# Four layers on one core: the small experts' gate and up weights as the stationary operand, and memsets on POOL between the transfers of five spreads

## The chip, the cores and the metric

The kernel runs on one core of a Trainium2 chip. The metric is the device time of one execution in microseconds; three executions of the kernel before took 1931.96, 1932.44 and 1936.04 us, so the median is 1932.44 us. The engines are named as in the profile: PE multiplies matrices, PEld is its loading of the stationary operand, DVE and ACT work on vectors, POOL issues the indirect transfers, SP issues the plain ones.

## What is computed

The reference is a network of four layers on x of 4 x 1024 x 128 in f32. Each layer has a token mixer and a feed-forward part, with a layer norm after each. What matters here are the routed parts of the second and fourth layer (L1 and L3), whose experts are small: 128 x 128 for gate, up and down. L2 routes too, with larger experts; it shares the transfers.

```python
# L1: 16 experts, 4 of a token, from the best groups
topk_idx, tw = _route(x, router_w, bias)
combine = (one_hot(topk_idx, 16) * tw[..., None]).sum(1)
h = einsum('td,edf->etf', x, gate_w)
u = einsum('td,edf->etf', x, up_w)
y = einsum('etf,efd->etd', silu(h) * u, down_w)
routed = einsum('etd,te->td', y, combine)
...
# L3: 32 experts, 4 of a token
h = silu(einsum('nd,ehd->neh', flat, gate_w)) * einsum('nd,ehd->neh', flat, up_w)
expert_out = einsum('neh,edh->ned', h, down_w)
sel = take_along_axis(expert_out, topk_idx[:, :, None], axis=1)
out = (sel * topk_scores[:, :, None]).sum(axis=1)
```

Both add a dense shared expert, and L2 routes every token to 2 of 8 experts.

## The kernel before

**Parts.** The 4096 tokens stand in SBUF as 32 tiles of 128. A routed layer takes them in parts: L1 as `a` and `r` (16 tiles each), L2 as `a` (16), `m` and `n` (8 each), L3 as `a` (16), `b` and `c` (8 each). "l1r" below is L1's part r.

**A routed part has four steps.** The router and `positions` give every pair of token and expert a row in a list sorted by expert, where each tile of 128 rows has one expert; the tiles' experts are the integers `ids`. `spread` (L1373) writes each tile of x to its rows in HBM: per tile and choice one indirect transfer from POOL, so 64 for 16 tiles of 4 choices and 32 for 8 tiles of 4 or 16 of 2. `small_experts` (L1781) goes through the list in groups of four tiles. `collect` (L1441) gathers the results back with indirect transfers (`yt`), and DVE adds them into x with the router's weight (L1452).

**A group of the small experts.** `gathered` loads four tiles of rows with SP (`xg`), and waits for all transfers of the spread. PE transposes them (`tp`), ACT copies that out (`xgT`). In `up`, PE reads the four experts' numbers into registers, and multiplies with the tile `xgT` stationary and 256 columns of the weights moving: gate and up of one tile in one product (`gu`, tokens on the partitions). ACT takes silu of the gate half (`sg`), DVE multiplies with the up half (`hg`). `turn` transposes `hg` on PE, DVE copies that out (`hT`, L173). `down` multiplies `hT` with the down weights (`yp`), ACT or DVE copies out (`yg`), and SP writes to the list of results. The weights of all experts of a layer lie in SBUF (`wall`, in the trace `ld`), loaded long before their use. Groups are pipelined: `up(g+1)`, `turn(g)`, `inputs(g+2)`, `down(g-1)` in one turn of the loop. There are 18 groups in l1a, 18 in l1r, 20 in l3a, 12 in l3b and 12 in l3c. A list can be longer than these; `rest_of` puts the further groups behind a branch on its length.

**What sets the order.** Each stage is a generator that yields its estimated time; `mix` (L242) runs a main one and a side one together, and sets the side's instructions in each engine's queue behind the latest of the main's. So the small experts of l1a run beside L0's and L1's work on the other half of the tokens, those of l1r beside L2's routing and the l2a spread, those of l3a beside L3's mixer for b, its routing and its spread, those of l3b and l3c beside the gathers of the part before.[...]

**The spreads that wait.** Under `spaced(..., 1, 2, 1.45)` an indirect transfer waits until the one two before it has landed (`before`, L1345), and the plan reckons 1.45 us for each. This holds for the spreads of l1r, l2a, l2m, l2n and l3a, and for some gathers; the spreads of l1a, l3b and l3c are not spaced. `indirect` (L1325) also keeps each transfer behind the last two of other lists on POOL (`self.moved`).

Of the kernel before, what the change touches and what calls it, by code (L numbers as in the profile page):

```python
# [14 lines left out]
AF = mybir.ActivationFunctionType  # L15
ALU = mybir.AluOpType
# [4 lines left out]
P = 128  # L21
# [3 lines left out]
BLK = 512  # L25
# [49 lines left out]
class Kernel:  # L75
    def __init__(self, ctx, tc, ins, out, cols, consts, rows):
        self.tc, self.nc, self.ins, self.out = tc, tc.nc, ins, out
        self.count = itertools.count()
        nc = self.nc
        self.const = self.pool(ctx, "const")  # L80
        self.small = self.pool(ctx, "small", 3)
        self.routes = self.pool(ctx, "routes")
        self.side = self.pool(ctx, "side", 2, space=PSUM)
        dram = self.pool(ctx, "dram", space=DRAM)

        self.cols_t = self.load(self.const, ins["cols"])
        self.cst_t = self.load(self.const, ins["consts"])
        self.x = self.tile(self.const, [P, NT, D], "x")
        self.xT = self.tile(self.const, [P, NT * P], "xT")
        nrow = ins["rows"].shape[1]  # L90
        self.rows_t = self.tile(self.const, [P, nrow], "rows")
        nc.gpsimd.dma_start(out=self.rows_t, in_=ins["rows"].to_broadcast([P, nrow]))
        self.col = {k: self.cols_t[:, a:b] for k, (a, b) in cols.items()}
        self.cst = {k: self.cst_t[:, a:b] for k, (a, b) in consts.items()}
        self.row = {k: self.rows_t[:, a:b] for k, (a, b) in rows.items()}
        self.ident = self.cst["ident"]
        self.eps = self.tile(self.const, [P, 1], "eps")
        nc.vector.memset(self.eps, LN_EPS)
# [1274 lines left out]
    def spread(self, lay, part, k):  # L1373

        pos, _, _, done, _ = self.route[lay + part.name]
        rows = self.lists[lay, part.name][0]
        for t in range(part.nt):
            for i in range(k):
                ins = self.indirect(
                    apart=done,  # L1380
                    out=rows, out_offset=bass.IndirectOffsetOnAxis(ap=pos[:, t, i : i + 1], axis=0),
                    in_=self.x[:, part.order[t], :], in_offset=None,
                )
                done.append(ins)
            yield (self.step * k,)
        self.listed.add(lay + part.name)

# [11 lines left out]
            )  # L1399
        return xg  # L1400

    def experts_of(self, ids, g, ne):
        _, es = self.nc.values_load_multi_w_load_instructions(
            ids[0:1, g * 4 : g * 4 + 4], engines=[mybir.EngineType.PE], min_val=0, max_val=ne - 1,
            skip_runtime_bounds_check_because="clamped to the last expert",
        )
        return es
# [370 lines left out]
        cp = self.pool(ctx, "l1fw")  # L1778
        return self.load(cp, self.ins["l1_w"])

    def small_experts(self, lay, ne, part, wall, held=None):  # L1781

        nc = self.nc
        pos, wk, ids, done, used = self.route[lay + part.name]
# [2 lines left out]
        with ExitStack() as ctx:  # L1787
            gp = self.pool(ctx, lay + "fg" + part.name, 3)
            ps = self.pool(ctx, lay + "fpe" + part.name, 2, space=PSUM)
            ng = tl // 4  # L1790
            xgTs, ess, hs, hTs = {}, {}, {}, {}

            def inputs(g):
                xg = self.gathered(gp, rows, g, done, part.nt * K3)
                xgTs[g] = self.tile(gp, [P, BLK], "xgT")
                self.transposes(ps, xgTs[g], [xg[:, i, :] for i in range(4)], on_act=True, tag="tp")

            def up(g):
                es = ess[g] = self.experts_of(ids, g, ne)
                xgT = xgTs.pop(g)  # L1800
                h = hs[g] = self.tile(gp, [P, 4, P], "hg")
                for c in range(2):
                    pg = self.tile(ps, [P, 2, 2, P], "gu")
                    for i in range(2):
                        self.mm(
                            pg[:, i].rearrange("p a f -> p (a f)"),
                            xgT[:, (2 * c + i) * P : (2 * c + i + 1) * P],
                            wall[:, bass.ds(es[2 * c + i] * (3 * P), 2 * P)],
                        )
                    sg = self.tile(gp, [P, 2, P], "sg")  # L1810
                    nc.scalar.activation(sg, pg[:, :, 0, :], AF.Silu)  # L1811
                    nc.vector.tensor_tensor(h[:, 2 * c : 2 * c + 2, :], sg, pg[:, :, 1, :], ALU.mult)  # L1812

            def turn(g):
                h = hs.pop(g)
                hT = hTs[g] = self.tile(gp, [P, BLK], "hT")
                self.transposes(ps, hT, [h[:, i, :] for i in range(4)], on_act=False, tag="tp")

            def down(g):
                es, hT = ess.pop(g), hTs.pop(g)  # L1820
# [12 lines left out]
                return marks  # L1833

            def rest(g):
                inputs(g)
                up(g)
                turn(g)
                down(g)


            inputs(0)
            inputs(1)
            up(0)
            for g in range(ng + 1):
                if g + 1 < ng:
                    up(g + 1)
                if g < ng:
                    turn(g)
                if g + 2 < ng:  # L1850
                    inputs(g + 2)
                marks = down(g - 1) if g else ()
                if g == ng:
                    while held and (got := self.queued(held)):
# [368 lines left out]
```

## Time and profile before

| | us |
|---|---|
| median of three executions | 1932.44 |
| the profiled execution | 1937.33 |
| its span, first to last instruction | 1935.5 |
| busy: PE, DVE, ACT, POOL | 1541.5, 1199.2, 900.6, 690.3 |
| l1a experts: first row loaded to last product | about 366 to 457 |
| l1r experts | about 746 to 836 |
| l3a experts | about 1596 to 1712 |
| l3b experts | about 1743 to 1796 |
| l3c experts | about 1816 to 1869 |

The granted PE clock was 0.896 over the whole. A row of a group gives the line, the engine, the operation, what it writes and reads, the count, the busy time and the mean of one; `x8` on a timeline row means eight of the kind one after the other. An f32 product appears as two records on PE. A line can be that of a helper: L161 is every product, L169 every transpose, L1327 every indirect transfer. In brackets stands how long the engine was idle before, and what released it. POOLq, ACTq, PEldq and SPq are the sequencers of these engines: register loads, branches and transfers' issues.

### The profile page before, as it was taken

What the parts mean: (1) busy time and instruction counts of PE and PEld (TensorE: products, weight loads), DVE (VectorE), ACT (ScalarE), POOL (GpSimd) and SP (SyncE); (2) the same over time, 40 slices, a digit from 0 to 9 for tenths busy, and PEclk for the clock granted to TensorE, in tenths of its full rate; (3) what the DMA queues carried; (4) which work ended last, traced back from release to release, by engine and by line L of the source; (5) the groups of instructions that cost most, each with busy time, mean ns of one, the idle gap of its engine ahead of it and who ended that gap; (6) DMA issues with size and microseconds to landing.
All of it is one profiled execution on the core that took longest, in us unless ns stands there. A gap on an engine that the chain in (4) does not pass through costs nothing. (4 is left out here: it accounts for less than half of the span.)

```text
span 1935.5 us, 27095 instructions
## 1 busy us (share of the span) xinstructions
PE 1541.5 (80%) x9025; PEld 920.8 (48%) x9025; DVE 1199.2 (62%) x3491; ACT 900.6 (47%) x1349; POOL 690.3 (36%) x670
## 2 busy tenths in 40 slices
PE   7885677597847887989977878798798998999850
PEld 3332433385423345856632232333355757768650
DVE  8998698465766664635564565546442446866383
ACT  5876265243324554423336756564532236644330
POOL 2000148604630660265443000030536430567775
PEclk9897688798978998999988988898988999989985
DMA  9990002244430113632241000000452213425452
GB/s 297 288 288 10 1 17 86 87 126 133 159 129 18 60 63 129 183 96 73 78 137 32 1 1 1 2 23 1 159 213 83 66 28 93 141 68 167 122 147 61
DMA packets 215530, 187.10 MB, mean 97 GB/s; under 512 B 16528, under 2 KB 194064, under 8 KB 214864
## 3 DMA queue, kind: packets, MB, share of 16 engines
q1 hardware_dynamic: 194672, 142.29, 23.6%
q0 software_dynamic: 20704, 42.86, 7.3%
q8 instruction: 84, 1.38, 0.3%
q14 instruction: 70, 0.57, 0.1%
HBM read 88.49 MB, written 96.60 MB: 96 GB/s over the span
## 5 line engine op out<-in xcount | busy, mean ns | idle before, releaser
L1081 ACT ACTIVATE pr<-sc 128x1024 f32<-128x1024 f32 x288 | 279.4, 1021 | 175.2 <-PE sc L161 174.8
L161 PE MATMUL sc<-qm,kT 32*128 32x512 f32 (+3 forms) x1536 | 197.7, 559 | 16.7 <-ACT pr L1081 16.7
L161 PE MATMUL s<-pr,va 128*32 128x512 f32 (+3 forms) x1536 | 167.5, 532 | 19.0 <-DVE x L1019 10.2
L161 PE MATMUL gu<-ld,xgT 128*128 x640 | 165.1, 400 | 10.2 <-DVE hg L1812 5.9
L1087 DVE TENSOR_TENSOR pr<-pr,ld 128x512 f32<-128x512 f32 (+1 forms) x160 | 91.7, 581 | 105.6 <-ACT pr L1081 105.4
L161 PE MATMUL gu<-wall,xgT 128*128 x304 | 148.2, 612 | 2.0 <-ACT xgT L171 2.0
L161 PEld LDWEIGHTS sc<-qm,kT 32*128 32x128 f32 x1536 | 83.7, 194 | 112.4 <-issue 61.1
L161 PEld LDWEIGHTS gu<-ld,xgT 128*128 128x128 f32 x640 | 119.5, 198 | 34.7 <-DVE hg L1812 6.1
L1812 DVE TENSOR_TENSOR hg<-sg,gu 128x256 f32<-128x256 f32 x160 | 66.0, 417 | 92.0 <-ACT sg L1811 91.6
L173 DVE COPY hT<-tp 128x512 f32<-128x512 f32 x118 | 80.9, 686 | 66.2 <-PE tp L169 66.2
L1567 ACT ACTIVATE sg<-gu 128x512 f32<-128x512 f32 x76 | 45.4, 597 | 144.7 <-PE gu L161 143.6
L1811 ACT ACTIVATE sg<-gu 128x256 f32<-128x256 f32 x160 | 61.3, 385 | 107.7 <-PE gu L161 79.8
L171 ACT COPY xgT<-tp 128x512 f32<-128x512 f32 x99 | 58.0, 586 | 99.9 <-PE tp L169 99.8
L1327 POOL DMA_INDIRECT l1ra<-x,posl1a x64 | 79.8, 1246 | 61.3 <-DVE peq L1321 42.0
L1327 POOL DMA_INDIRECT l1rr<-x,posl1r x64 | 65.4, 1022 | 100.9 <-DVE posl1r L1302 70.8
L169 PEld LDWEIGHTS tp<-ld,hg 128*128 128x128 f32 x624 | 77.4, 141 | 49.0 <-issue 32.5
L1569 DVE TENSOR_TENSOR hg<-sg,gu 128x512 f32<-128x512 f32 x76 | 51.8, 682 | 78.9 <-ACT sg L1567 78.8
L1327 POOL DMA_INDIRECT l2rm<-x,posl2m x16 | 15.7, 983 | 236.8 <-DVE peq L1320 230.1
L169 PE MATMUL tp<-ld,hg 128*128 128x128 f32 x624 | 96.4, 275 | 3.7 <-DVE hg L1812 2.0
L1327 POOL DMA_INDIRECT l3ra<-x,posl3a x64 | 63.7, 996 | 93.3 <-DVE usedl3a L1315 51.0
L161 PEld LDWEIGHTS s<-pr,va 128*32 128x32 f32 x1536 | 37.1, 113 | 122.6 <-issue 78.4
L161 PE MATMUL yp<-ld,hT 128*128 x640 | 86.1, 276 | 2.3 <-DVE mv L197 1.5
(447 smaller groups left out, 3439.1 us busy)
## 6 DMA issues: line engine op xcount, KB each, us to landing
wall<-wall SPq DMA_DIRECT2D x16, 768.0 KB, 7.8
l3ra<-zero SPq DMA_DIRECT2D x1, 6144.0 KB, 25.5
ld<-in_l_w SPq DMA_DIRECT2D x2, 3072.0 KB, 10.6
wall<-we SPq DMA_DIRECT2D x24, 256.0 KB, 2.1
ld<-in_l_w SPq DMA_DIRECT2D x1, 6144.0 KB, 20.6
l1ra<-zero SPq DMA_DIRECT2D x1, 5120.0 KB, 19.6
l1rr<-zero SPq DMA_DIRECT2D x1, 5120.0 KB, 23.1
xg<-l3ra SPq DMA_DIRECT2D x20, 256.0 KB, 2.9
```

Of the source, the lines that this page charges most:

```text
L161: return self.nc.tensor.matmul(out, lhsT, rhs, start=start, stop=stop)
L169: nc.tensor.transpose(pt[:, k * P : (k + 1) * P], s, self.ident)
L171: nc.scalar.copy(dst, pt[:, : n * P])
L173: nc.vector.tensor_copy(dst, pt[:, : n * P])
L1081: nc.scalar.activation(pr, sc[h], AF.Exp)
L1087: nc.vector.tensor_tensor(d, d, cst["tril"].unsqueeze(1).unsqueeze(1).to_broadcast([P, 2, n, P]), ALU.mult)
L1327: ins = self.nc.gpsimd.indirect_dma_start(**kw)
L1567: nc.scalar.activation(sg, gu[:, 0, :], AF.Silu)
L1569: nc.vector.tensor_tensor(h, sg, gu[:, 1, :], ALU.mult)
L1811: nc.scalar.activation(sg, pg[:, :, 0, :], AF.Silu)
L1812: nc.vector.tensor_tensor(h[:, 2 * c : 2 * c + 2, :], sg, pg[:, :, 1, :], ALU.mult)
```

## The change

There are two parts. In the small experts of L1 and L3, gate and up swap operands. A new step `held(g)` copies the gate and up weights of a group's four experts out of `wall` into a tile `wc` of 128 x 4 x 256 (three buffers): the first two with ACT, the other two with DVE, each after reading its two experts' numbers into its own registers. `up` then multiplies with 128 columns of `wc` stationary and the tile `xgT` moving, once for gate and once for up, so that features come out on the partitions, and the result has the layout that `down` needs: `turn`, its transposes and its copy are gone. The loop has one turn less, and `held` runs two groups ahead. PE reads the experts' numbers in `up` as before, and uses them in `down` alone.

In `spread`, when it is spaced, a memset of a 128 x 384 tile of bytes on POOL follows each transfer, and is entered in `self.moved`, so that later transfers queue behind it. Nothing reads the tile.

```diff
+        self.idle = self.tile(self.const, [P, 384], "idle", mybir.dt.uint8)
...
                 done.append(ins)
+                if self.spacing:
+                    stay = self.nc.gpsimd.memset(self.idle, 0)
+                    self.tc.add_manual_dep(
+                        stay.ins, ins.ins.name,
+                        mybir.DependencyInfo(mybir.DependencyClass.NoSync, mybir.DependencyReason.DATA),
+                        reason="queued behind",
+                    )
+                    self.moved.append(stay.ins.name)
             yield (self.step * k,)
...
-    def experts_of(self, ids, g, ne):
+    def experts_of(self, ids, g, ne, engine=mybir.EngineType.PE, first=0, count=4):
         _, es = self.nc.values_load_multi_w_load_instructions(
-            ids[0:1, g * 4 : g * 4 + 4], engines=[mybir.EngineType.PE], min_val=0, max_val=ne - 1,
+            ids[0:1, g * 4 + first : g * 4 + first + count], engines=[engine], min_val=0, max_val=ne - 1,
...
+            def held(g):
+
+                wc = wcs[g] = self.tile(gp, [P, 4, 2 * P], "wc", bufs=3)
+                for n, (eng, copy) in enumerate((
+                    (mybir.EngineType.Activation, nc.scalar.copy), (mybir.EngineType.DVE, nc.vector.tensor_copy),
+                )):
+                    es = self.experts_of(ids, g, ne, eng, 2 * n, 2)
+                    for i in range(2):
+                        copy(wc[:, 2 * n + i, :], wall[:, bass.ds(es[i] * (3 * P), 2 * P)])
+
             def up(g):
                 es = ess[g] = self.experts_of(ids, g, ne)
+                wc = wcs.pop(g)
...
                     for i in range(2):
-                        self.mm(
-                            pg[:, i].rearrange("p a f -> p (a f)"),
-                            xgT[:, (2 * c + i) * P : (2 * c + i + 1) * P],
-                            wall[:, bass.ds(es[2 * c + i] * (3 * P), 2 * P)],
-                        )
+                        for j in range(2):
+                            self.mm(
+                                pg[:, j, i, :], wc[:, 2 * c + i, j * P : (j + 1) * P],
+                                xgT[:, (2 * c + i) * P : (2 * c + i + 1) * P],
+                            )
                     sg = self.tile(gp, [P, 2, P], "sg")
-                    nc.scalar.activation(sg, pg[:, :, 0, :], AF.Silu)
-                    nc.vector.tensor_tensor(h[:, 2 * c : 2 * c + 2, :], sg, pg[:, :, 1, :], ALU.mult)
-
-            def turn(g):
-                h = hs.pop(g)
-                hT = hTs[g] = self.tile(gp, [P, BLK], "hT")
-                self.transposes(ps, hT, [h[:, i, :] for i in range(4)], on_act=False, tag="tp")
+                    nc.scalar.activation(sg, pg[:, 0], AF.Silu)
+                    nc.vector.tensor_tensor(h[:, 2 * c : 2 * c + 2, :], sg, pg[:, 1], ALU.mult)
...
-                    pm = self.mm(py[:, i, :], hT[:, i * P : (i + 1) * P], wall[:, bass.ds(es[i] * (3 * P) + 2 * P, P)])
+                    pm = self.mm(py[:, i, :], h[:, i, :], wall[:, bass.ds(es[i] * (3 * P) + 2 * P, P)])
...
+            held(0)
+            held(1)
             inputs(0)
             inputs(1)
             up(0)
-            for g in range(ng + 1):
+            for g in range(ng):
+                if g + 2 < ng:
+                    held(g + 2)
                 if g + 1 < ng:
                     up(g + 1)
-                if g < ng:
-                    turn(g)
                 if g + 2 < ng:
                     inputs(g + 2)
-                marks = down(g - 1) if g else ()
-                if g == ng:
+                marks = down(g)
+                if g + 1 == ng:
```

More of the change, by code (lines that the diff above doesn't have):

```diff
@@ L1779, in l1_wall, with small_experts @@
         return self.load(cp, self.ins["l1_w"])
-    def small_experts(self, lay, ne, part, wall, held=None):
+    def small_experts(self, lay, ne, part, wall, ahead=None):
         nc = self.nc
@@ L1790, in small_experts @@
             ng = tl // 4
-            xgTs, ess, hs, hTs = {}, {}, {}, {}
+            xgTs, ess, hs, wcs = {}, {}, {}, {}
             def inputs(g):
@@ L1804, in up @@
                     for i in range(2):
-                        self.mm(
-                            pg[:, i].rearrange("p a f -> p (a f)"),
-                            xgT[:, (2 * c + i) * P : (2 * c + i + 1) * P],
-                            wall[:, bass.ds(es[2 * c + i] * (3 * P), 2 * P)],
-                        )
-                    sg = self.tile(gp, [P, 2, P], "sg")
-                    nc.scalar.activation(sg, pg[:, :, 0, :], AF.Silu)
-                    nc.vector.tensor_tensor(h[:, 2 * c : 2 * c + 2, :], sg, pg[:, :, 1, :], ALU.mult)
-            def turn(g):
-                h = hs.pop(g)
-                hT = hTs[g] = self.tile(gp, [P, BLK], "hT")
-                self.transposes(ps, hT, [h[:, i, :] for i in range(4)], on_act=False, tag="tp")
+                        for j in range(2):
[3 more added lines that the diff above has]
+                            )
+                    sg = self.tile(gp, [P, 2, P], "sg")
+                    nc.scalar.activation(sg, pg[:, 0], AF.Silu)
+                    nc.vector.tensor_tensor(h[:, 2 * c : 2 * c + 2, :], sg, pg[:, 1], ALU.mult)
             def down(g):
-                es, hT = ess.pop(g), hTs.pop(g)
+                es, h = ess.pop(g), hs.pop(g)
                 py = self.tile(ps, [P, 4, D], "yp")
                 for i in range(4):
-                    pm = self.mm(py[:, i, :], hT[:, i * P : (i + 1) * P], wall[:, bass.ds(es[i] * (3 * P) + 2 * P, P)])
+                    pm = self.mm(py[:, i, :], h[:, i, :], wall[:, bass.ds(es[i] * (3 * P) + 2 * P, P)])
                 yg = self.tile(gp, [P, 4, D], "yg")
@@ L1835, in rest @@
             def rest(g):
+                held(g)
                 inputs(g)
                 up(g)
-                turn(g)
                 down(g)
+            held(0)
+            held(1)
             inputs(0)
@@ L1844, in small_experts @@
             up(0)
-            for g in range(ng + 1):
+            for g in range(ng):
+                if g + 2 < ng:
+                    held(g + 2)
                 if g + 1 < ng:
                     up(g + 1)
-                if g < ng:
-                    turn(g)
                 if g + 2 < ng:
                     inputs(g + 2)
-                marks = down(g - 1) if g else ()
-                if g == ng:
-                    while held and (got := self.queued(held)):
+                marks = down(g)
+                if g + 1 == ng:
+                    while ahead and (got := self.queued(ahead)):
                         self.now += got[0]
```

## The prediction

> **What bounds the kernel now.** I read the table of busy time by stage first, cut at the first and last row of each list of experts, since the change touches only those stages and the spreads. Its columns are the stretch, its length, busy time of PE, PE's weight loads, DVE, ACT and POOL, then granted clock, DMA share and GB/s.
>
> ```profile
> 366.00:458.00 92.00, 78.38 (x504) 69.58 (x504) 62.15 (x135) 32.84 (x69) 17.68 (x8) 0.93 0.35 104
> 746.00:836.00 90.00, 75.06 (x457) 66.28 (x457) 49.68 (x196) 34.39 (x69) 18.20 (x19) 0.92 0.60 190
> 1596.00:1712.00 116.00, 103.42 (x620) 83.73 (x620) 86.92 (x294) 70.51 (x137) 35.01 (x32) 0.98 0.38 113
> 1743.00:1796.00 53.00, 47.95 (x296) 41.80 (x295) 30.94 (x76) 24.50 (x50) 40.37 (x42) 0.97 0.58 171
> 1816.00:1869.00 53.00, 45.41 (x288) 40.53 (x288) 30.49 (x84) 24.95 (x50) 38.91 (x41) 0.97 0.64 171
> 1869.00:1936.00 67.00, 0.00 (x0) 0.00 (x0) 34.50 (x153) 2.08 (x7) 39.89 (x38) 0.51 0.27 72
> ```
>
> The five stages are l1a, l1r, l3a, l3b and l3c with 18, 18, 20, 12 and 12 groups. PE is the fullest engine in each; in the last 67 us it does nothing. One steady group of l3a on PE (start, length, instruction):
>
> ```profile
> 1648.81 1.97 PE L161 MATMUL gu<-ld,xgT 128*128 x8
> 1650.61 0.60 PE L169 MATMUL tp<-ld,hg 128*128 128x128 f32 x4
> 1651.05 0.60 PE L169 MATMUL tp<-ld,xg 128*128 128x128 f32 x4
> 1651.48 1.06 PE L161 MATMUL yp<-ld,hT 128*128 x8
> 1652.38 0.43 PE L161 MATMUL gu<-ld,xgT 128*128 x1
> ```
>
> From start to start: gate and up 1.80 us, the transposes of h 0.44, those of the input 0.43, down 0.90: 3.57 us a group, no gap. Each f32 product is two records.
>
> Whether a stage's gain reaches the end depends on POOL, which issues every scatter and gather. At the end of l1r:
>
> ```profile
> 854.42 0.96 POOL L1327 DMA_INDIRECT l2ra<-x,posl2a  x1 [0.30 <-DMA l2ra<-x,posl2a]
> 859.60 4.01 SPq L1392 DMA_DIRECT2D xg<-l2ra  x3
> 860.41 1.83 PE L161 MATMUL py<-ld,hs 128*128 128x128 f32 x14 [0.63 <-DVE hs L764]
> 862.58 0.63 PE L169 MATMUL tp<-ld,xg 128*128 128x128 f32 x4 [0.34 <-DMA xg<-l2ra]
> ```
>
> PE ends its last product before l2's first experts at 862.2 and waits 0.34 us for rows whose scatter ended just before: PE and the l2a spread are in balance there. And at the end of the kernel, the gathers of l3:
>
> ```profile
> L1327 POOL DMA_INDIRECT yt<-l3ya,posl3a x64: 943/945/1185, 1712.8 to 1833.7; - x64
> L1327 POOL DMA_INDIRECT yt<-l3yb,posl3b x32: 943/945/1003, 1836.4 to 1875.3; - x32
> L1327 POOL DMA_INDIRECT yt<-l3yc,posl3c x32: 944/945/3440, 1877.6 to 1920.3; - x32
> ```
>
> With the 32 scatters of l3c between them these are 160 transfers in 207.5 us, 1.30 each, where 0.96 of work and 0.30 of issue make 1.26. From 1712.8 on POOL is the bound, and it starts when l3a is made. So a faster l3b or l3c is worth nothing; an earlier end of l3a moves the end one for one.
>
> **The change part by part.**
>
> *PE.* Gate and up become 16 records of 128 columns in place of 8 of 256. Down is 8 such records in 0.90 us, weight loads hidden, so 16 take 1.80: nothing gained or lost. The four transposes of h go: 0.44 us a group, and with them DVE's copy hT (0.69 us, 128x512 from PSUM) and its two hand-overs. A PE-bound group goes from 3.57 to 3.13 us.
>
> *The copies.* ACT gets two 128x256 copies a group: its row on SBUF of that size is `lg`, 0.42 us; so 0.83. DVE gets two; its copies of 128x256 elements (`sv`, `em`) take 0.29, so 0.59, less than the 0.69 that leaves. Each engine also reads two expert numbers into registers, once a group. PE reads four such in these rows:
>
> ```profile
> L1403 PEldq TENSOR_LOAD <-idsl3a x20: 328/332/792, 1600.1 to 1698.2; - x20
> L1418 ACTq TENSOR_LOAD <-usedl1a x1: 467/467/467, 455.2 to 455.2; - x1
> ```
>
> [...] I take the row, and half of that load as hidden, since at 455.2 ACT's load ran under its copy yg. The copies are made one or two groups ahead of their use, so they reach PE only where ACT's or DVE's queue is full.
>
> *l1a.* PE is full in nearly all of it: 18 x 0.44 = 7.9, less two groups that stand at a bump, plus about 0.6 of shorter drain: 7.5 us. The gathers of l1ya start as soon as l1a ends (459.3, after waiting for its writes), so this passes on.
>
> *l1r.* The first seven groups are held by transfers: the second-layer weights load with DMA at 0.60 of the stage. The other eleven save 11 x 0.44 = 4.8. But the l2a spread starts behind about five of them on DVE, so some 2 us earlier; PE then waits for it. Before the memsets the stage is worth 2, not 4.8.
>
> *l3a.* 20 x 0.44 = 8.8 if PE bound it throughout. In these two slices ACT does, and gets 0.83 to 1.2 us a group in about four groups, 4.5 us:
>
> ```profile
> 1634.00:1644.00 10.00, 7.80 (x46) 6.60 (x45) 3.92 (x11) 8.34 (x14) 0.00 (x0) 0.83 0.18 52
> 1664.00:1674.00 10.00, 6.74 (x44) 5.57 (x44) 7.27 (x22) 9.48 (x20) 7.56 (x9) 1.00 0.59 173
> ```
>
> I take +4, between -2 (ACT late everywhere) and +9.
>
> *The memsets.* 192 on POOL, one behind each transfer of the five spreads that wait for landings (l1r 64, l2a 32, l2m and l2n 16 each, l3a 64). No row has 384 one-byte elements; the nearest are POOL's `zero`, 128 elements, 0.23 us, and `keep`, 1024, 0.96: 0.83 ns an element, so 0.42 us by elements, 0.18 if four bytes go at once. What a transfer then costs more lies between 0.06 (the memset fills the 0.30 us of issue) and 0.45 (it stands beside it). For a lower end, POOL's memset `zero` at the start overlapped the DMA behind it by 0.09 us. I take 0.15. Most of it is covered: these transfers already wait for the landing two before. Going through the starts in the rows and lengthening only steps that no landing set, l1r's 64 end 6.5 us later (22 at 0.45), l2a's 32 end 0.9 later (4.9), l3a's and l2n's 80 end 2.9 later (10.8). Cover: l1r's last lands 19 us before its first rows are loaded at 745.5, l3a's some 88 us before 1596. l2a has none: 2 - 0.9 leaves 1. A gain from a memset has no row to speak for it; I put it at nothing.
>
> [...]
>
> **Sum**, on the profiled execution's own time of 1937.3 us (span 1935.5 and 1.8 around it): 7.5 + 1 + 4 - 1.5 = 11, so 1926.3. That execution lay 4.9 us above the median of the runs; the same 11 off 1932.4 gives 1921.4, rounded to 1921.5.
>
> **The rivals.**
>
> *POOL falls behind its plan* (slower). At 0.45 a memset, l1r's spread ends 22 us later against 19 of cover: 3 lost. The l2a spread ends 4.9 - 2 = 3 late, and PE waits for it. The l3a spread ends 10.8 late, and with it the gathers of l2m behind it in POOL's queue (1508.6 to 1531.4); their adds stand on DVE from 1526 to 1536 ahead of the experts' products, which then wait up to 10. With 1.5 at the end that is 17.5 against gains of 11.5: 1938.5. It decides from about 0.40 a memset. For it: nothing in the plan's step of 1.45 us a transfer allows for a memset, and what a memset costs between two transfers has no row. Against: the cover named above.
>
> *ACT takes it back* (no change). If its load and copies are exposed in all 20 groups of l3a (22 us on 70.5 busy, in a queue that PE waits on), l3a gives -2 and l1a's 7.5 is halved by late input copies: 1932.4 - 3.7 + 2 + 1.5 - 1 = 1931. Against: ACT has 33 of 92 us in l1a.
>
> *All of it passes* (faster still): 7.9 + 4.8 + 8.8, nothing lost at the end, the l2a spread earlier with the experts: 1911. For it: the chain from h to down loses a copy and a PE pass, so PE's short gaps close too. Against: the balance at 862.
>
> **How the numbers follow.** Likeliest case 0.55, 1921.5, its own range 1914 to 1928. POOL behind 0.20; ACT 0.13; all of it 0.12. What can be told from no change is 0.2%, 3.9 us, so the ACT case counts as the same. Faster: 0.53 of the likeliest, 0.12, and little else, 0.65. Slower: 0.20. Same: 0.15. Eight in ten: from the all-passes case to beyond the POOL case, 1909 to 1941.
>
> **What would show it.** Right: steady groups of l1a and l3a at about 3.1 us on PE; no transposes of hg in these stages; first gather of l3ya near 1702 and the last still 207 us behind it; PE waiting some us for xg of l2ra. Wrong: transfers of l1rr a steady 1.7 us apart; DVE standing before x<-yt adds of l2m; ACT at nine tenths through l3a with PE waiting for wc; l3's gathers stretched beyond 1.35 each.

## The result

Four executions of the changed kernel took 1947.09 to 1957.0 us, median 1955.11; the kernel before, beside it, 1933.13 in the median of four. The ratio is 1.0108, 95% interval 1.0091 to 1.0125: slower by 1.1%, where 0.6% faster was forecast, and outside the range. Ratios, here and below, compare executions of each kernel within 1.5% of its quickest; where executions spread by 2 to 3%, that leaves out about half of the kernel before's. The profiled execution took 1954.32 us, its span 1952.5, at a granted clock of 0.890.

The busy time by stage of the changed kernel, with the columns of the table in the prediction (l1a, l1r, l3a with its first loads, and the last 67 us):

```profile
364.00:459.00 95.00, 72.86 (x564) 68.43 (x564) 64.15 (x153) 42.15 (x102) 17.39 (x8) 0.92 0.37 104
743.00:857.00 114.00, 88.85 (x679) 74.71 (x680) 53.31 (x232) 54.76 (x116) 26.39 (x38) 0.88 0.49 153
1573.00:1730.00 157.00, 139.78 (x900) 108.70 (x898) 104.06 (x365) 97.29 (x206) 49.73 (x49) 0.99 0.32 93
1885.00:1952.00 67.00, 0.00 (x0) 0.00 (x0) 27.16 (x112) 1.48 (x5) 41.72 (x39) 0.50 0.23 60
```

In l1a PE has 5.5 us less to do than before (72.86 against 78.38), and yet the stage ends no earlier: PE now waits. One steady group of l1a of the changed kernel in the timeline, PE and ACT alone, and one of the two rows of sg:

```profile
407.22 2.05 PE L162 MATMUL gu<-xgT,wc 128*128 128x128 f32 x16 [0.29 <-ACT xgT L172]
...
409.11 0.60 PE L170 MATMUL tp<-ld,xg 128*128 128x128 f32 x4
...
409.31 0.38 ACT L1831 ACTIVATE sg<-gu 128x256 f32<-128x256 f32 x1 [0.51 <-PE gu L162]
...
409.55 1.06 PE L162 MATMUL yp<-ld,hg 128*128 x8
...
410.13 0.41 ACT L1815 COPY wc<-ld 128x256 f32 x1 [0.43 <-issue]
...
410.44 0.58 ACT L172 COPY xgT<-tp 128x512 f32<-128x512 f32 x1
...
410.92 0.41 ACT L1815 COPY wc<-ld 128x256 f32 x1
...
411.07 1.30 PEld L162 LDWEIGHTS gu<-xgT,wc 128*128 128x128 f32 x11 [0.66 <-ACT xgT L172]
411.07 1.38 PE L162 MATMUL gu<-xgT,wc 128*128 128x128 f32 x10 [0.47 <-ACT xgT L172]
```

The next gate and up start at 411.07, 3.85 us after the last. The input's transposes are over at 409.7, but ACT copies them out only from 410.44: it first reads two expert numbers (0.66 us in this group, 0.37 of it while sg runs) and makes one weight copy. In the kernel before the same copy on ACT, in the group of l3a that the prediction shows, was this:

```profile
1651.68 0.59 ACT L171 COPY xgT<-tp 128x512 f32<-128x512 f32 x1 [0.49 <-PE tp L169]
```

It follows its transposes (1651.05 to 1651.65) at once, and ends 0.11 us ahead of the gate and up at 1652.38. The transposes of h are gone as predicted (no tp<-hg row is left in these stages), 16 products of 128 columns take about the time of the former 8 (2.05 us for 1.97), and what PE saved it waits for xgT. Steady groups, from start to start of gate and up, are 3.9 us in l1a, l1r and l3c, against 3.54 before. The loads, which I had priced at PE's 0.33 (shortest, median and longest in ns):

```profile
L1412 ACTq TENSOR_LOAD <-idsl1a x18: 482/494/803, 360.7 to 437.5; - x18
L1412 DVEq TENSOR_LOAD <-idsl1a x18: 519/531/1060, 373.7 to 441.6; - x18
L1412 PEldq TENSOR_LOAD <-idsl1a x18: 328/332/755, 382.2 to 450.8; - x18
```

The groups on POOL, all of it, of the changed kernel (count, busy, mean ns, idle before and its causes):

```profile
L1387 POOL MEMSET idle<- 128x384 uint8 x192 | 84.1, 438 | 0.1
L1328 POOL DMA_INDIRECT l1rr<-x,posl1r x64 | 65.0, 1016 | 85.0 <-DVE posl1r L1303 70.8 <-issue 9.7 <-DMA l1rr<-x,posl1r 4.5
```

and the same list of the kernel before:

```profile
L1327 POOL DMA_INDIRECT l1rr<-x,posl1r x64 | 65.4, 1022 | 100.9 <-DVE posl1r L1302 70.8 <-DMA l1rr<-x,posl1r 23.8 <-issue 6.4
```

A memset takes 0.44 us. The landings that the l1r spread waited for shrink from 23.8 to 4.5 us, but it runs 106.0 us from first to last start where it ran 94.6; the l2a spread 54.0 for 49.3, l3a's 161.3 for 151.8. At the l2a spread's end PE now waits 3.7 us for its first rows, 0.34 before:

```profile
877.87 1.83 PE L162 MATMUL py<-ld,hs 128*128 128x128 f32 x14 [0.63 <-DVE hs L765]
...
883.39 0.80 PE L170 MATMUL tp<-ld,xg 128*128 128x128 f32 x4 [3.70 <-DMA xg<-l2ra]
```

The end of the kernel is as before: the last 160 transfers take 207.3 us (207.5).

```profile
L1328 POOL DMA_INDIRECT yt<-l3ya,posl3a x64: 944/947/1405, 1730.0 to 1851.2; - x64
...
L1328 POOL DMA_INDIRECT yt<-l3yc,posl3c x32: 942/944/948, 1898.6 to 1937.3; - x32
```

Where the two profiled executions part, by the same rows in both (us from the span's start):

| | before | changed | later by |
|---|---|---|---|
| first gate and up of l1a | 379.6 | 375.0 | -4.6 |
| first gather of l1ya | 459.3 | 459.2 | -0.1 |
| first transfer of l1rr | 629.0 | 634.9 | 5.9 |
| first gate and up of l1r | 758.1 | 774.4 | 16.3 |
| first gather of l1yr | 855.7 | 879.1 | 23.4 |
| first gate and up of l3a | 1601.0 | 1624.4 | 23.4 |
| first gather of l3ya | 1712.8 | 1730.0 | 17.2 |

l1a started earlier and ended at the same time; l3a made up 6 us. Most of the loss lies between 635 and 879, in the l1r spread, the layer 2 mixer beside it and l1r. Suspicion therefore fell on two things: the copies on ACT (theory C) and the memsets (theory M).

### The profile page after: what moved, and what is told of

It is laid out like the page before. It is cut to its first block, busy times and chain, and to the rows that moved or that the text cites. A ratio compares the mean times of both kernels' runs of the same rounds, so it can differ in the third digit from the quotient of the medians.

```text
span 1952.5 us, 28304 instructions
## 1 busy us (share of the span) xinstructions
PE 1521.4 (78%) x9345; PEld 919.7 (47%) x9345; DVE 1192.1 (61%) x3571; ACT 945.7 (48%) x1509; POOL 773.5 (40%) x862
## 5 line engine op out<-in xcount | busy, mean ns | idle before, releaser
L162 PE MATMUL gu<-xgT,wc 128*128 128x128 f32 x1280 | 169.5, 285 | 33.9 <-ACT xgT L172 16.7
L162 PE MATMUL s<-pr,va 128*32 128x512 f32 (+3 forms) x1536 | 166.2, 528 | 17.2 <-DVE x L1020 7.1
L162 PEld LDWEIGHTS gu<-xgT,wc 128*128 128x128 f32 x1280 | 155.5, 197 | 49.1 <-ACT xgT L172 24.1
L162 PE MATMUL gu<-wall,xgT 128*128 x304 | 152.5, 628 | 5.2 <-DVE hg L1578 3.2
L162 PE MATMUL yv<-s,wbd 128*128 128x512 f32 x128 | 71.5, 680 | 28.1 <-DVE s L368 28.1
L1328 POOL DMA_INDIRECT yt<-l1ya,posl1a x64 | 69.0, 1078 | 49.7 <-issue 17.1
L162 PE MATMUL yp<-ld,hg 128*128 x640 | 85.9, 277 | 1.3 <-DVE hg L1832 0.9
L1387 POOL MEMSET idle<- 128x384 uint8 x192 | 84.1, 438 | 0.1
L692 POOL TENSOR_TENSOR g<-g,pw 128x1024 f32<-128x1024 f32 x2 | 6.7, 3330 | 195.5 <-DVE l1h L689 195.5
```

Source lines behind the costliest of these rows:

```text
L162: return self.nc.tensor.matmul(out, lhsT, rhs, start=start, stop=stop)
L692: (tt if beside else nc.gpsimd.tensor_tensor)(rows(g[0]), rows(g[0]), steps(pw[:, 0, :]), ALU.mult)
L1328: ins = self.nc.gpsimd.indirect_dma_start(**kw)
L1387: stay = self.nc.gpsimd.memset(self.idle, 0)
```

## First runs: the parts alone

The swap alone is the changed kernel without the memsets, the memsets alone the kernel before with them. Two more kernels are the swap alone with its copies moved: in e3 ACT's stand behind its copy of the input, in e4 DVE makes all four:

```diff
 # e3: held(g + 2) after down(g), and for ACT's two copies
+                        self.tc.add_manual_dep(cp.ins, turned[g].ins.name, NoSync)
 # e4, in held
-                for n, (eng, copy) in enumerate(((Activation, nc.scalar.copy), (DVE, nc.vector.tensor_copy))):
-                    es = self.experts_of(ids, g, ne, eng, 2 * n, 2)
+                es = self.experts_of(ids, g, ne, mybir.EngineType.DVE)
+                for i in range(4):
+                    nc.vector.tensor_copy(wc[:, i, :], wall[:, bass.ds(es[i] * (3 * P), 2 * P)])
```

> The changed kernel without its memsets: only the swapped operands with the copies on ScalarE and VectorE. Theory C (the copies: ACT's register load of 0.5 us and first copy of 0.41 us stand ahead of the copy of the turned input, which had no slack): the loss stays, 1945 to 1955 us, ratio 1.006 to 1.012, with l1a still at 3.7 to 4.0 us a group. Theory M (the memsets cost it: the l1r spread ended 17 us later and the l2a spread 23 us later with them): the loss goes, 1925 to 1932 us, ratio 0.996 to 1.000, with the first product of l1r back near 755 us after the start.

> The kernel before, with the memsets alone. Theory C: within 0.3% of the kernel before, 1930 to 1937 us, because the spread of l1r has 19 us of cover and the lag of the others is hidden; the l1r spread takes 106 us in place of 95. Theory M: 1945 to 1955 us, with the experts of l2a reached 10 to 20 us later.

> As the swap alone, but in each turn ACT's register load and its two copies stand behind its copy of the turned input (xgT) of the same group in ACT's queue. Theory C in its strong form (only the order on ACT is wrong): groups of l1a fall from 3.7 to 4.0 us to about 3.2, and the time is 8 to 12 us under that of the swap alone. Rival Q (ACT's queue as a whole is too full: silu 0.77, input 0.58, output 0.58, copies 0.82, load 0.5 = 3.25 us a group, over the 3.13 of PE): groups of l3a stay at 3.5 us or above, and the delay moves to silu and from there to the product that reads hg; no more than 4 us gained.

> As the swap alone, but all four copies and one load of four expert numbers on VectorE, none on ScalarE. Theory C and rival Q: ACT's copy of the turned input follows its transposes at once again; VectorE has 4 x 0.29 + 0.5 = 1.7 us more and 0.69 less a group, so l1a falls to about 3.2 to 3.4 us a group, and the time is 5 to 12 us under the swap alone. Rival P (it is the 128-column products with their weight loads that take longer on PE): groups stay at 3.7 to 4.0 us.

On the chip of these runs the kernel before itself took 2269 us, 17% more than on the first one. To it: swap alone 1.0129 (1.0049 to 1.0209), memsets alone 0.9406 (0.9336 to 0.9476), e3 1.0073 (1.0045 to 1.0101), e4 1.0049 (1.0017 to 1.0080). The medians of all executions give the swap alone 1.012 and the memsets 0.940, but e4 0.999, so e4's sign is open. That the memsets make a kernel 6% faster I had not foreseen. What ACT did in the swap alone while POOL issued the l1r spread (all of ACT's rows from 664 to 747; start, length, idle before):

```profile
664.87 1.94 ACT L1081 ACTIVATE pr<-sc 128x1024 f32<-128x1024 f32 x2 [1.51 <-DVE o L1002]
674.03 1.94 ACT L1081 ACTIVATE pr<-sc 128x1024 f32<-128x1024 f32 x2 [7.22 <-remote]
704.45 0.59 ACT L171 COPY oT<-s 128x512 f32<-128x512 f32 x1 [28.48 <-remote]
746.49 1.02 ACT L1081 ACTIVATE pr<-sc 128x1024 f32<-128x1024 f32 x1 [41.46 <-remote]
```

"Remote" means that no instruction's end explains the wait. The product that oT waits for ended at 678.45; its signal is recorded at 704.42, 26 us later. Through all this POOL issued transfers 1.27 us apart; the spread's last started at 742.2, and the next signal from PE came at 746.47. Call a signal of PE, ACT or DVE late when the next record of it comes over 1 us after its instruction's end. There are none in the two profiles of the first chip; in the swap alone there are 356, 1940 us together, all but 17 of them while POOL was issuing transfers. (Several signals can share a record: DVE has 2718 records for 3004 signals there. Each signal is counted, so the sum is not time lost.) In the l1r spread there were 18, 271 us together, in the swap alone, and 7, 15 us together, with memsets.

The groups of l1a, where POOL issues no transfers, can be compared all the same. Steady ones take 3.54 us with the memsets alone, 3.9 in the swap alone, 3.5 in e3 and 3.2 in e4. So the predicted 3.13 is what PE does when ACT has no copies (3.16 in e4); behind the input's copy they still cost 0.3 (rival Q), and the 128-column products are not the cause (rival P).

The same on another chip of that kind (before 2250 us):

> The changed kernel without its memsets, on another chip if one is given, since the first chip for it held up the signals between the engines while POOL issued. Theory C (the copies and register loads on ACT cost the time): steady groups of l1a at 3.9 us as in the changed kernel, and 1.003 to 1.008 of the kernel before. Theory M (the memsets cost it): 0.994 to 1.000 of the kernel before.

> The kernel before with the memsets alone. Theory C: 0.998 to 1.003 of the kernel before where signals are prompt; the spread of l1r takes 11 us longer under its 19 us of cover. Theory M: 1.006 to 1.012.

> All four copies and one register load a group on DVE, none on ACT, and no memsets. Theory C: steady groups at 3.2 us, and 0.992 to 0.998 of the kernel before, that is 5 to 15 us faster. Rival D (DVE's added 1.2 us of copies a group delays the work of the side generators on DVE by as much as PE gains): 0.998 to 1.003.

The ratios are 1.0094 (1.0040 to 1.0149), 0.9506 (0.9457 to 0.9554) and 1.0021 (0.9957 to 1.0086); by the medians of all executions 1.007, 0.948 and 0.995. On such chips the memsets gain and the swap with copies on ACT loses; what copies on DVE do is within the noise. For the first chip that decided nothing.

## Holding the signals out of it

If POOL's unbroken issue holds the signals up, a memset behind every transfer, gathers too, should free them, and the swap can then be compared without them. In `indirect`, with the memset of `spread` gone:

```diff
         self.moved_by = max(self.moved_by, self.now) + self.step
+        stay = self.nc.gpsimd.memset(self.idle, 0)
+        self.tc.add_manual_dep(stay.ins, ins.ins.name, behind, reason="queued behind")
+        self.moved.append(stay.ins.name)
         return ins
```

> The kernel before with a memset of 128x384 bytes on POOL behind every indirect transfer, the gathers and the unspaced spreads too. Theory S (on such a chip the signals between PE, ACT and DVE are held up while POOL issues transfers 1.27 us apart, and the memset's 0.44 us lets them through): the held-up signals, some 1400 us in sum with memsets in five spreads alone, fall below 300 us, and the time is 40 to 110 us under that of the memsets alone, 2020 to 2090 us. Rival T (only the write transfers of spreads hold signals up, gathers stretch for a reason of their own): no more than 20 us under it. On a chip with prompt signals: 40 to 70 us slower than the kernel before, as the last 160 transfers take 0.4 us more each.

> As the paced kernel, with the swapped operands and the copies on ACT and DVE of the change. Theory C: 8 to 25 us above the paced kernel; steady groups of l1a at 3.9 us against 3.54. Theory M (the swap gains and the memsets cost): 5 to 12 us below it.

> As the paced kernel, with the swapped operands and all four copies on DVE. Theory C: steady groups at 3.2 us and 5 to 15 us below the paced kernel. Rival D (DVE's copies cost the other work as much as PE gains): within 4 us of it.

> The changed kernel itself on the same chip as the others. If the two parts of the change add: where signals are held up, the memsets alone gave 0.941 to 0.951 and the swap alone 1.009 to 1.013, so 0.95 to 0.963 of the kernel before; where signals are prompt, 1.009 to 1.013 as recorded.

On a third chip of that kind (before 2272.8 us): paced 2015.4 us (0.8888, 0.8812 to 0.8964), its late signals 570 us together, where memsets in five spreads had left 1670 (e2); paced swap 2027.9; paced with DVE copies 2017.4, executions from 2013 to 2028; the changed kernel 2163.1 (0.9530, 0.9442 to 0.9617), inside what was worked out from the parts. Theory S holds in time, a little beyond its forecast of 2020 to 2090; the late signals, expected below 300 us, are not all gone. That the pause lets the signals through is argued from this, and not seen. In the paced world the swap costs 12.5 us (four executions from 2027.5 to 2028.8 against five from 2013 to 2026), and copies on DVE cost nothing but gain nothing (rival D). So theory C had the upper hand here.

## What in the swap costs: order, load or copy

Four paced kernels: the swap with one more yield, which gives the planner as many turns as before the change (of 5813 records of products outside the routed experts, 36 then stand elsewhere in PE's order in the trace, 159 without it); DVE copies with the first two groups' on ACT and that yield; a memset of a third of the size, in the kernel before; and the swap with copies of fixed experts, so without loads on ACT and DVE, which leaves the choice of the weights out.

```diff
 # h1, h2: after the loop
+            yield (3.7,)
 # h2, in held
+                on_act = g < 2
+                es = self.experts_of(ids, g, ne, mybir.EngineType.Activation if on_act else mybir.EngineType.DVE)
 # h3
-        self.idle = self.tile(self.const, [P, 384], "idle", mybir.dt.uint8)
+        self.idle = self.tile(self.const, [P, 128], "idle", mybir.dt.uint8)
 # h4, in held
-                        copy(wc[:, 2 * n + i, :], wall[:, bass.ds(es[i] * (3 * P), 2 * P)])
+                    (nc.scalar.copy if i < 2 else nc.vector.tensor_copy)(wc[:, i, :], wall[:, i * (3 * P) : i * (3 * P) + 2 * P])
```

> The paced kernel with the swap and its copies on ACT and DVE, and one more yield of 3.7 us at the end of each small_experts, so that the planner counts as many turns as before the change (25 products outside the experts stand elsewhere instead of 91). Theory O (the neighbours' order is a large part of the loss): 4 to 8 us under the paced swap, about 2021 to 2024 us. Theory C alone (all of the loss is in the experts' own groups): within 2 us of the paced swap, 2026 to 2030 us.

> The paced kernel with the swap, all four copies on DVE from the third group on, those of the first two groups on ACT (idle 37 us before the stage), and the further yield. The first step of l1a was 6.1 us with DVE copies, because they stood behind DVE's other work, against 3.2 in the paced kernel, which ate the 10 x 0.35 us of the steady groups. If that and the order are what was lost: first step 3 to 4 us, and 5 to 12 us under the paced kernel, 2003 to 2011 us. Rival D (DVE's copies cost the neighbours the rest): within 4 us of the paced kernel.

> The paced kernel with memsets of 128x128 bytes in place of 128x384, some 0.2 us in place of 0.44, so transfers some 1.4 us apart. If any pause lets the held-up signals through: as few late signals as in the paced kernel, and 20 to 50 us under it, since the last 160 transfers, POOL-bound, come closer together: 1965 to 1995 us. If the pause has to be long: late signals between the 600 us in sum of the paced kernel and the 1900 us without, and 30 us or more above the paced kernel.

> The paced swap without register loads on ACT and DVE: the copies take four fixed experts, so gate and up are computed with the wrong weights; sizes and counts are the same. If the load (median 0.5 us on ACT) is what makes ACT late: steady groups of l1a fall from 3.9 to 3.3 to 3.4 us. If the copy itself does (0.41 us in front of the turned input): 3.6 to 3.8 us. In time 3 to 10 us under the paced swap.

The chip was one like the first: the kernel before took 1931.65 us, and each of the four profiles has two late signals at most, none over 1.9 us. In time: h1 2023.8, h2 2013.5, h3 1957.9, h4 2005.9 us. The question that h3 asked, how short a pause frees held-up signals, stays open, as nothing was held up here; the run shows instead what pacing costs where nothing needs it, 26 us with memsets of 0.225 us.

Between h1 and h4 lie 18 us, and they differ in the loads and in the one yield, so the 18 us are not the loads' alone. The groups tell more. A steady one of h4:

```profile
413.60 0.60 PE L170 MATMUL tp<-ld,xg 128*128 128x128 f32 x4
413.80 0.38 ACT L1822 ACTIVATE sg<-gu 128x256 f32<-128x256 f32 x1 [1.54 <-PE gu L162]
...
414.08 0.40 ACT L1806 COPY wc<-ld 128x256 f32<-128x256 f32 x1
...
414.38 0.59 ACT L172 COPY xgT<-tp 128x512 f32<-128x512 f32 x1
...
415.02 2.05 PE L162 MATMUL gu<-xgT,wc 128*128 128x128 f32 x16
```

The first copy still stands ahead of xgT, but without the load it is done by the time the transposes are, and the group takes 3.3 us. So of the 0.75 us that a group with copies on ACT takes beyond 3.16, the loads cost 0.6 and the copy 0.15; and as groups with a load on DVE alone take 3.16 (e4), it is ACT's load that costs. h1 is 4 us under g2, which ran on the other kind of chip; this says little of the order. Nor was the paced kernel run on this chip, so there is nothing to set h2's time against.

## The parts alone, where signals are prompt

The last three runs, on a chip of the first kind (before 1932.26 us, 23 executions), are the swap alone and the memsets alone again, and h2 without any memset:

> The changed kernel without its memsets. Theory C (register loads in front of the copies on ACT, and the neighbours' order): where signals are prompt 12 to 18 us over the kernel before, ratio 1.006 to 1.009. Theory M (the memsets, by the later end of the l1r and l2a spreads): within 4 us of the kernel before. Where signals are held up: 1.009 to 1.013 as before.

> The kernel before with the memsets alone. Theory C: where signals are prompt 3 to 9 us over the kernel before (what is left of the 22 us), as the l2a spread ends 4.6 us later; theory M: 15 to 22 us over it. Where signals are held up: 0.94 to 0.95.

> The swap with all four copies on DVE, those of the first two groups of a stage on ACT, one more yield, and no memsets. If the loads on ACT and the order were the whole loss: 3 to 12 us under the kernel before, ratio 0.994 to 0.998. Rival D (DVE's copies cost the neighbours what PE gains): 0.998 to 1.003.

| | median us | ratio | interval |
|---|---|---|---|
| swap alone (i1) | 1931.7 | 1.0005 | 0.9987 to 1.0022 |
| memsets alone (i2) | 1945.7 | 1.0088 | 1.0060 to 1.0116 |
| DVE copies, no memsets (i3) | 1922.9 | 0.9954 | 0.9936 to 0.9972 |

The first two together make 1.0093, the changed kernel 1.0108 (1.0091 to 1.0125): the loss is the memsets', 17 us by the ratio (12 to 22) and 13.5 by the medians, and the swap alone is worth nothing (2.5 us faster to 4 slower). For chips with prompt signals theory C falls and M stands. And the third beats both kernels, by 9 us (5 to 12) to the kernel before. One of its steady groups in l1a:

```profile
397.49 2.00 PE L161 MATMUL gu<-xgT,wc 128*128 128x128 f32 x16
...
399.33 0.60 PE L169 MATMUL tp<-ld,xg 128*128 128x128 f32 x4
...
399.96 0.59 ACT L171 COPY xgT<-tp 128x512 f32<-128x512 f32 x1
...
400.66 2.00 PE L161 MATMUL gu<-xgT,wc 128*128 128x128 f32 x16
```

The group takes 3.17 us: xgT follows its transposes at once again.

How the memsets cost it can be read where swap alone and changed kernel, whose PE queues are the same, pass the same norm in layer 2's mixer. First the swap alone: DVE's norm begins and ends, then the product of PE that waits for it, and a later one.

```profile
726.04 0.17 DVE L180 TENSOR_SCALAR rstd<-ve 128x4 int32<-128x4 int32 x1
...
728.83 1.11 DVE L213 TENSOR_SCALAR x<-x,mv,rstd 128x128 f32<-128x128 f32 x4
...
729.33 1.01 PE L169 MATMUL s<-ld,x 128*128 128x128 f32 x4 [0.79 <-DVE x L213]
...
732.25 1.14 PE L161 MATMUL sc<-qm,kT 32*128 32x512 f32 x8
```

The l1r spread is over by then, its last transfer having started at 721.4. In the changed kernel it still runs:

```profile
738.10 0.43 POOL L1387 MEMSET idle<- 128x384 uint8 x1
738.10 0.46 DVE L181 TENSOR_SCALAR rstd<-ve 128x4 int32<-128x4 int32 x1
...
738.70 0.96 POOL L1328 DMA_INDIRECT l1rr<-x,posl1r  x1 [0.17 <-issue]
...
739.19 0.44 DVE L187 TENSOR_SCALAR nwt<-nwt 128x4 f32<-128x4 f32 x1
...
742.06 0.93 PE L170 MATMUL s<-ld,x 128*128 128x128 f32 x4 [1.54 <-DVE x L214]
...
745.81 2.09 PE L162 MATMUL sc<-qm,kT 32*128 32x512 f32 x8
```

One operation of 0.17 us ends with the memset after 0.46, another with the transfer after 0.44. PE waits 1.54 us in place of 0.79; and then the clock is at half for 6.8 us, where in the swap alone it is full, and the same eight products take 2.09 us for 1.14. The granted clock beside it, 10 us long, in the swap alone and in the changed kernel (the last but two column):

```profile
728.00:738.00 10.00, 9.21 (x108) 5.36 (x107) 5.70 (x18) 7.57 (x11) 0.00 (x0) 1.00 0.01 1
```

```profile
743.50:753.50 10.00, 10.00 (x88) 5.26 (x81) 2.88 (x7) 5.39 (x7) 0.00 (x0) 0.66 0.27 79
```

Earlier in the same spread stands another such wait of PE, first in the swap alone, then in the changed kernel, where one scalar operation that takes 0.17 us took 0.71 beside a transfer:

```profile
651.68 1.33 PE L169 MATMUL s<-ld,x 128*128 128x128 f32 x4 [4.21 <-DVE x L213]
```

```profile
652.82 0.71 DVE L182 TENSOR_SCALAR rstd<-rstd 128x4 int32<-128x4 int32 x1
...
657.88 1.50 PE L170 MATMUL s<-ld,x 128*128 128x128 f32 x4 [4.68 <-DVE x L214]
```

The half clock that goes with it lasted 3.4 us in the one and 13.7 in the other. Between 630 and 860 the clock stood at half for 47.8 us in the changed kernel and 28.2 in the swap alone, for 37.5 with the memsets alone and 28.7 before.

What comes ahead of half clock can be worked out from the traces. In the clock records of these profiles the stretches begin and end on a grid of 3.41 us. Cut on this grid, between 400 and 1860, the window just ahead of a half-clock stretch has PE idle for 45% or more in 26 of 29 cases in the changed kernel, 26 of 33 in the swap alone; of the some 315 windows at full clock with full clock behind them, 8 and 5 have. Ahead of 743.77 PE was idle for 1.62 us of 3.41; in the swap alone no window of that norm has more than 1.04. So half clock followed there on a wait longer by 0.75 us; that the wait brings it is inferred from these counts. In the earlier pair it is not the length alone: 4.21 us filled one whole window, 4.68 fell on two (1.83 and 2.86 us), and why the clock then stayed at half through two windows in which PE worked all but 0.13 us is not explained.

How often operations of DVE are stretched can be counted. Against the shortest of the same tile and shape in the same trace, 23 of the 447 DVE operations that start in the five spreads are over 0.15 us longer in the changed kernel, 7.7 us in all; 5 of 402, 1.1 us, in the swap alone; 22 of 444, 6.8 us, with the memsets alone; 4 of 408, 0.8 us, before. About half of them end within 0.1 us of an instruction of POOL. Of those beside a memset in the changed kernel 14 of 24 TENSOR_SCALARs were stretched, and 1 of 94 TENSOR_TENSORs.

Where the time goes shows in two pairs of profiles. From the first transfer of l1rr to the first gather of l1yr it is 226.7 us before and 236.8 with the memsets alone, 228.8 in the swap alone and 244.2 in the changed kernel: 10 and 15 us more with memsets. In the second pair, product by product: of the 19 us between the two executions, 5.4 had arisen before the first memset ran, so they belong to the execution and not to the change; 10.2 come up from the start of the l1r spread to the end of the mixer beside it, in steps of 4.2, 2.5 and 3.6 around pieces of half clock, and 4.6 by the end of the l2a spread, where PE waits 3.7 us for its first rows (0.98 in the swap alone) and then works at half clock; the rest of the way gives 1 back. The profiled execution of the memsets alone was the fastest of its six (1939.9 to 1955.2) and shows only 2.6 us in all: it came to the spread 3.6 us early and made up 4 us behind it. How the cost divides between stretched operations, the clock and the later spreads in an average execution was not settled, and no run has a pause on POOL that leaves DVE alone.

## Why the prediction was wrong

Two terms of the sum failed. The swap, put at a gain of 12 us (7.5 + 2 + 4 - 1.5), brought nothing with its copies on ACT and DVE: by place in ACT's queue they reach PE. The memsets, put at 1 us, cost 13.5 to 17: in the profiles beside stretched operations of DVE and half clock after PE's waits for them, and through the l2a spread, which grew five times as much as forecast.

*The bound, and PE's group.* Right as far as PE goes: with the copies off ACT a group takes 3.16 us (3.13 predicted).

*"So they reach PE only where ACT's or DVE's queue is full."* This is the first step that failed. ACT was busy 42 of 95 us in l1a, far from full. What counts is place, not fullness: the load and one copy stand between the last sg and xgT, and xgT had 0.1 us of slack. By the first gather of l1ya, the 7.5 us of l1a became 0.1 in the changed kernel and 0.9 in the swap alone; with the copies on DVE the stage ended 8.1 us earlier.

*The register load.* I took the row of 0.33, PE's, and half of it as hidden. On ACT and DVE it is 0.49 and 0.53. A row of the same instruction on another engine was not a row for this one. The half taken as hidden was about right in the group shown. h4, without these loads on ACT and DVE (and with one yield less), is 18 us faster than h1, and its groups are 0.6 us shorter.

*l1r, worth 2 at most because l2a's spread is in balance with PE.* The balance is real: in i3 l1r starts 5.7 us early, and layer 1's gathers behind the l2a spread only 2.5; PE waits 2.7 us for xg of l2ra. In the swap alone the stage lost instead of gaining, 3.9 us from first to last gate and up: PE waits 5.6 us for xgT there, 0.2 before, and 5.3 for rows, 3.6 before.

*l3a +4, between -2 and 9.* From the first gate and up to l3ya's first gather the stage went from 111.8 us to 105.6 in the changed kernel, 105.3 in the swap alone and 102.5 in i3. Right, and somewhat more than I took; ACT's rival, that it takes l3a back, did not happen.

*The memsets, one microsecond.* The estimate by elements, 0.42 us, fits the 0.44. What a transfer costs more, I put at 0.15, and there it is about 0.31: 0.13 of the 0.30 us of issue run under the memset, no more. The l1r spread grew by 11.4 us, between the 6.5 for 0.15 and the 22 for 0.45. The l2a spread grew by 4.7 us, where 0.9 was forecast against 2 of cover, and PE's wait for its rows is part of the loss. That term was too small. The larger step that failed is another: I asked only what the later transfers hold up. The l1r spread's cover held, as its last transfer at 740.9 was in time for the rows at 743.3, which PE took only from 772. Of the 19 us between the changed kernel's profile and the swap alone's, 10.2 came up beside that spread, around pieces of half clock. In the five spreads 23 of 447 of its operations were stretched in the changed kernel, 5 of 402 in the swap alone; beside POOL's instructions three scalar ones of 0.17 us took 0.44, 0.46 and 0.71, and about half of those stretched ended with one of POOL's. PE waited for DVE, at 742 for 1.54 us in place of 0.79. And ahead of 26 of the 29 stretches at half clock between 400 and 1860 PE had been idle for 45% or more of 3.41 us; between 630 and 860 such stretches lasted 3.4, 6.8 and 13.7 us in the changed kernel.

*The end, -1.5.* No run shows the 1.5 us that the sum takes off for the end of the kernel. From l3ya's first gather to the span's end there were 222.7 us before, 222.5 in the changed kernel, 223.9 in the swap alone: the changed kernel lost nothing there. That POOL alone sets it was right.

*The rival "POOL falls behind its plan".* Its sign was right, and its time, 1938.5, the nearest, 17 us short. Of its path one piece came true: the l2a spread ends late and PE waits 3.7 us (3 forecast). Two of its signs came too, the transfers of l1rr 1.68 us apart on average and DVE standing before the adds of l2m (8.2 us, not seen before); but l1r's cover held, and l3a's experts started no later against l1yr than before (23.4 us late at both).

The 11 us of the sum come near the 9 measured for a change that was not made, the swap with copies on DVE and no memsets. In part that is luck: in i3's profile, against the one before, l1a's 8.1 us are down to 2.5 by the first gather of l1yr, and l3a gives 9.3.

## What to carry to other kernels

A helper instruction moved to an engine "with room" can cost what stands behind it in that engine's queue, however idle the engine is on average: here ACT was busy 42 of 95 us in l1a, and its load and copies cost 0.75 us a group. Look for the operation that has no slack, and put the register load and the copies behind it or on another engine. An instruction that pads one engine can go with longer operations on another: beside POOL's memset one of DVE took 0.46 us for 0.17. Where PE waited for DVE, 0.75 us more of waiting was followed here by 6.8 us at half clock, by estimate some 3 us of time, as eight products took 2.09 us there for 1.14. A change that wins or loses by one chip's manner should be timed on more than one before its cause is argued.

## What was not expected of the hardware

On three of the five chips of the experiments the signals between PE, ACT and DVE were recorded up to 65 us late (f3), nearly always while POOL issued indirect transfers close together, and the kernel before took 2250 to 2273 us in place of 1932. Memsets of 0.44 us in five spreads brought it down by 5 to 6%, behind every transfer by 11%; on a chip without late signals those in five spreads cost 0.9%, and ones half as long behind every transfer 1.5% (h3). Why chips differ in this was not found, nor how short a pause is enough.

A register load of two numbers took 0.48 us or more on ACT and 0.52 on DVE (minimum of 18), while four numbers on DVE took less, in the profile of i3:

```profile
L1403 DVEq TENSOR_LOAD <-idsl1a x16: 340/356/651, 371.6 to 438.4; - x16
```

What makes the shorter load the longer one was not tried.
